# Two graph-attention layers: neighbours of 32 nodes gathered four to a tile and summed on column tiles of TensorE

## The chip, the core and the metric

The kernel runs on one core of a Trainium2 chip. The core has five engines that run side by side and wait for one another through semaphores: TensorE (PE, with its weight loads shown as PEld), VectorE (DVE), ScalarE (ACT), GpSimd (POOL) and SyncE (SP, which here only issues transfers). Sixteen DMA engines move data between DRAM and the on-chip memory SBUF. TensorE writes to a second on-chip memory, PSUM, which DVE and ACT can read. The metric is the time of one execution in microseconds, taken as the median of several runs.

## The reference

Both layers are graph attention over the same 2708 nodes with 1024 features, in f32. About 17 entries per row of the adjacency matrix are set, and a row attends only to those.

```python
def layer0(x, adj):
    f = x @ Wf + bf
    g = x @ Wg + bg
    e = relu(f @ g.T)
    a = softmax(where(adj > 0, e, NEG), axis=1)
    return a @ (x @ W + bW)

def layer1(x, adj):
    h = x @ W1
    e = leaky_relu(h @ a1 + (h @ a2).T, 0.2)
    a = softmax(where(adj > 0, e, NEG), axis=1)
    return relu(a @ h)

x = layernorm(x + layer0(x, adj))
x = layernorm(x + layer1(x, adj))
```

## The kernel before

The kernel turns the dense adjacency matrix into lists of neighbours and computes only with these. It uses that sums and products can be exchanged: f . g = x_i (Wf Wg^T) x_j plus terms with the biases, so with M = Wf Wg^T a node needs one row F = x M + c, and a score is the product of F with the row x_j of a neighbour; likewise a @ (x W) is (a @ x) W. So each layer gathers rows of x (or of the table T1 of layer 1), and multiplies by a weight matrix once per node.

*Lists (L141 to L235).* The 2708 rows are 22 blocks of 128. For each block the adjacency rows are loaded by SP, DVE multiplies them by a falling iota (L216), finds the eight largest of each of 20 segments (L220) and draws up to 40 neighbours out of these in five rounds (L224, L226). Meanwhile PE turns Wf and Wg and forms M (L200), and POOL and ACT form the products of the weights with the bias vectors and with a1 and a2 (L174, L175).

*Ranking (L237 to L298).* Nodes are sorted by their number of neighbours, so that a block needs no more places than its first node has: DVE and ACT compare every node's key with all the others (L264, L270), and POOL scatters each list to its rank in the DRAM tensor LD (L129). SP reads the ranked lists back into SL. `PLACES` says how many neighbours each block of 128 ranked nodes may have, 396 places in all. A check whether the lists fit is made here (L298 to L311); if it fails, a general path runs, which it does not for this input.

*Layer 0 (L486 to L598).* Every place is one indirect DMA of POOL (`gather_next`, L411): 128 rows of 4 KB, row p being the neighbour of node p; entries without a neighbour are out of bounds and are skipped. The tiles lie in a ring of 20 slots. A block (or half a block where it has over 20 places) is a unit. For each unit, DVE forms the score of each place as a product of the tile with F, summed along the row (`dots`, L520), `soft` (L418) makes the weights, and `add_up` (L449) sums the weighted tiles: some places on PE, as products with a diagonal 128x128 matrix of weights that ACT writes (`share`, L441), the others on DVE, one multiply-add each. `join` adds the two parts. The numbers `np0` and `np1` choose the split. A slot's next gather is issued behind the instruction that reads it last. `prepare` (L510) makes F of the block after next, `values` (L539) multiplies the sum by W, and `close` (L545) adds the residual, normalizes (`norm`, L347), forms the two products with u1 = W1 a1 and u2 = W1 a2 and scatters the row into T1.

*Layer 1 (L601 to L668).* The same with T1's rows, a ring of 28 slots, and scores that need only column D of the gathered row (`scores`, L610).

The order of the instructions on every engine in both layers is that of the code: each call is wrapped by `InOrder` (L42), so every engine works through its queue as written, and a waiting instruction holds up all that stand behind it on its engine. Since the wrapper makes these calls, the profile puts them all on L52; they are told apart by the tiles that they write and read.

## Time and profile before

| | before |
|---|---|
| median of three runs | 2166.41 us (2160.6 to 2173.15) |
| profiled execution | 2171.14 us |
| its span, first to last instruction | 2169.3 us |
| mean granted TensorE clock | 0.882 |
| busy PE, DVE, POOL, ACT | 1697.8, 1745.4, 1086.1, 461.2 us |
| moved by DMA | 501.03 MB |
| lists / ranking / start of layer 0 | 0 to 234 / 234 to 311 / 311 to 363 us |
| sums of layer 0 | 363 to 1433 us |
| between the layers | 1433 to 1501 us |
| layer 1 up to its last gather / end | 1501 to 2085 / 2085 to 2169.3 us |

The stages were read off the timeline. A line of a group names the engine and the operation, what it writes and reads (`out<-in`), how often (`x`), its busy time and mean duration, and how long its engine idled before it and for whom. `ring` is the ring of gathered tiles, `dg` a diagonal of weights, `acc` the sum on DVE, `j` the discarded product of a dot, `pm` and `pt` are PSUM tiles, `xT` and `yT` are turned rows.

### The profile page before, as it was taken

Reading aid. Unit: us, or ns where it says so; the run is one execution under the profiler, and the core shown is the slowest. Engines: PE = TensorE matmul, PEld = TensorE weight load, DVE = VectorE, ACT = ScalarE, POOL = GpSimd, SP = SyncE. Lnnn points to the kernel's source line nnn. Section 1 sums busy time; section 2 is a strip of 40 time slices with the busy share of each in tenths; the row PEclk is TensorE's granted clock in tenths of the full one; section 3 lists DMA queues with packets and bytes.
Section 4 is the critical chain, followed back from the end, with each engine's and each line's share of the span. In section 5 each row is a group of like instructions: output and inputs, shape, how many; then the busy total and the mean of one; then the engine's idle time right before and its main releaser. Section 6 shows DMA issues by size and latency. Waiting matters only on the chain.

```text
span 2169.3 us, 16547 instructions
## 1 busy us (share of the span) xinstructions
PE 1697.8 (78%) x4200; PEld 756.1 (35%) x4200; DVE 1745.4 (80%) x3089; ACT 461.2 (21%) x859; POOL 1086.1 (50%) x991
## 2 busy tenths in 40 slices
PE   2787217797788799999999999962385968886896
PEld 2343103343333334444444444320132433342442
DVE  8999836678778878989999989963677778886993
ACT  3223601111122012222222222210002212231331
POOL 4237244453453445554554454307676767775740
PEclk6799558898988899999999999975697979998998
DMA  6554027264654556765676566417898989998940
GB/s 250 202 199 162 4 89 290 82 245 164 228 205 163 199 205 250 273 249 210 235 269 259 203 233 241 149 60 276 273 362 328 350 314 378 379 371 309 378 167 34
DMA packets 143618, 501.03 MB, mean 231 GB/s; under 512 B 26040, under 2 KB 26376, under 8 KB 140806
## 3 DMA queue, kind: packets, MB, share of 16 engines
q0 software_dynamic: 125312, 424.80, 53.3%
q1 hardware_dynamic: 12088, 52.01, 6.4%
q10 hardware_dynamic: 6114, 23.07, 2.9%
q8 instruction: 36, 0.59, 0.1%
q14 instruction: 68, 0.56, 0.1%
HBM read 494.23 MB, written 33.80 MB: 243 GB/s over the span
## 4 chain that ended last, share of the span: by engine, by line
PE 42%; issue 9%; DVE 5%; another core or an unknown queue 3%; ACT 3%; DMA 3%; POOL 2%; POOLq 1%; DVEq 0%; ACTq 0%
PE pm L52 41%; DVE acc L52 2%; POOL ring L52 2%; DMA ring<-T,SL 1%; DVE j L52 1%; PE pt L52 1%; DMA more<-T,SL 1%; POOL more L52 1%; ACT F L52 1%; ACT L52 1%; POOLq L52 1%; DVE z L52 1%; DVE bst L52 0%; ACT z L52 0%
## 5 line engine op out<-in xcount | busy, mean ns | idle before, releaser
L52 POOL DMA_INDIRECT ring<-in_x_dram,SL x396 | 434.3, 1097 | 518.3 <-DVE acc L52 376.3
L52 PE MATMUL pm<-ring,dg 128*128 128x512 f32 x932 | 438.0, 626 | 157.1 <-ACT dg L52 79.1
L52 DVE SCALAR_TENSOR_TENSOR acc<-ring,sc,acc 128x1024 f32<-128x1024 f32 (+1 forms) x408 | 524.2, 1285 | 14.6
L52 DVE SCALAR_TENSOR_TENSOR j<-ring,F 128x1024 bf16<-128x1024 f32 (+1 forms) x396 | 483.7, 1222 | 22.6 <-PE pt L52 11.2
L52 PE MATMUL pm<-M,yT 128*128 128x512 f32 (+1 forms) x704 | 325.6, 622 | 73.8 <-ACT yT L52 57.1
L52 POOL DMA_INDIRECT ring<-T,SL x284 | 297.0, 1046 | 122.4 <-issue 77.5
L52 PE MATMUL pm<-Wt,xT 128*128 128x512 f32 (+1 forms) x704 | 329.5, 623 | 14.9 <-ACT xT L52 14.7
L52 PEld LDWEIGHTS pm<-ring,dg 128*128 128x128 f32 x932 | 186.2, 202 | 402.4 <-issue 312.5
L52 PE MATMUL pm<-M,xT 128*128 128x512 f32 (+1 forms) x704 | 316.8, 603 | 3.5 <-issue 3.0
L52 PEld LDWEIGHTS pm<-M,yT 128*128 128x128 f32 (+1 forms) x704 | 134.9, 195 | 251.5 <-issue 189.3
L52 PEld LDWEIGHTS pm<-Wt,xT 128*128 128x128 f32 (+1 forms) x704 | 132.4, 193 | 187.4 <-issue 167.6
L52 PEld LDWEIGHTS pm<-M,xT 128*128 128x128 f32 (+1 forms) x704 | 128.2, 187 | 166.3 <-issue 164.1
L52 POOL DMA_INDIRECT more<-T,SL x112 | 119.1, 1064 | 46.6 <-issue 30.0
L174 POOL TENSOR_TENSOR vp<-rows,vec 128x1024 f32<-128x1024 f32 x32 | 89.7, 2829 | 101.7 <-DMA rows<-in_L_gnn_Wg_dram 71.1
L52 ACT COPY xT<-pt 128x512 f32<-128x512 f32 (+1 forms) x88 | 46.9, 579 | 373.5 <-PE pt L52 233.3
L200 PE MATMUL pm<-WgT,WfT 128*128 128x512 f32 x256 | 117.1, 620 | 7.3 <-ACT M L202 6.9
L52 DVE TENSOR_TENSOR acc<-pm,acc 128x1024 f32<-128x1024 f32 x48 | 58.6, 1221 | 76.7 <-issue 47.4
L52 ACT ACT_TABLE_LOAD x79 | 101.4, 1283 | 67.9 <-DVE nm L52 49.6
L52 DVE SCALAR_TENSOR_TENSOR acc<-more,sc,acc 128x1024 f32<-128x1024 f32 (+1 forms) x82 | 105.3, 1284 | 2.9
L220 DVE MAX8 cand<-adj 128x8 f32<-128x136 f32 (+2 forms) x440 | 107.5, 281 | 0.0
L52 ACT COPY yT<-pt 128x512 f32<-128x512 f32 (+1 forms) x44 | 23.6, 570 | 327.3 <-PE pt L52 193.3
L52 ACT ACTIVATE dg<-ident,sc 128x128 f32<-128x128 f32 x258 | 81.3, 389 | 28.3 <-DVE sc L52 13.4
(126 smaller groups left out, 1317.5 us busy)
## 6 DMA issues: line engine op xcount, KB each, us to landing
adj<-in_adj_dram SPq DMA_DIRECT2D x21, 1354.0 KB
X1S<-z SPq DMA_DIRECT2D x21, 512.0 KB
x<-X1S SPq DMA_DIRECT2D x21, 512.0 KB
ring<-in_x_dram,SL POOLq DMA_INDIRECT x396
ring<-T,SL POOLq DMA_INDIRECT x284
rows<-in_L_gnn_Wf_dram ACTq DMA_DIRECT2D x8, 512.0 KB
rows<-in_L_gnn_Wg_dram ACTq DMA_DIRECT2D x8, 512.0 KB
rows<-in_L_gnn_W_dram ACTq DMA_DIRECT2D x8, 512.0 KB
```

The source lines that it names most:

```text
L52: return self.tc.keep_in_program_order(op(*args, **kwargs))
L174: nc.gpsimd.tensor_tensor(t, rows, vec, op=ALU.mult)
L200: nc.tensor.matmul(pm[:, 0, :], WfT[:, i, k * P:(k + 1) * P], WgT[:, i, :], start=(i == 0), stop=(i == KC - 1))
L220: nc.vector.max(cand[:n, s, :], k[:n, s * SEG:min((s + 1) * SEG, N)])
```

## The change

The nodes stay sorted by their number of neighbours, but the unit of the lists is now a group of 32 nodes (85 groups, 405 tiles in `TILES`), and a gathered tile holds four neighbours of each of them: row 32 q + i is a neighbour of node i. `sums` forms a group's weighted sum on PE alone: the stationary operand is a 128x32 matrix `st` (each row holds its weight in the column of its node), and the result goes to the 32 PSUM partitions that belong to the group, so the four groups of a block write to four different column tiles. Units of over 20 tiles (27 in layer 1) are cut into two units of two groups. DVE keeps the dots and writes `st`; it no longer sums. For the dots, F of a group's 32 nodes is written four times by ACT (`replicate`).

The ranks no longer come from comparing all keys: nodes fall into 11 classes by their number of tiles, counted by products with triangular and one-hot matrices, and the node of each rank is found by one-hot products (44 small ones). The lists go to DRAM unranked, block by block, and are gathered by group when they are needed (`load_lists`, 85 indirect DMAs).

Also changed: in the lists, ACT and POOL form the masked iota; the bias and a1/a2 products are formed on PE with broadcast columns, for which W1 is turned as well; weights are loaded by SP; the normalization takes its inverse root by three Newton steps on DVE and not by ACT's square root; z is one buffer; closing a block is spread over the next one by hooks in `sums`; PSUM holds two product tiles and one for the sums; layer 1's ring has 27 slots; the check of the lists comes at the end of layer 1.

```diff
-PLACES = [40, 26, 23, 22, 21, 20, 19, 19, 18, 18, 17, 17, 16, 16, 16, 15, 14, 14, 13, 12, 11, 9]
+
+TILES = [10] + [7] * 4 + [6] * 13 + [5] * 30 + [4] * 28 + [3] * 9
...
+    LD = dram.tile([N * Q, QT], I32, name="LD")
...
+    stack = const.tile([P, 32], F32, name="stack")
+    rep = const.tile([P, Q, 32], F32, name="rep")
...
+            def turned(w, k, dst):
+                t = stage.tile([P, D], F32, name="rows")
+                sp.dma_start(t, w[k * P:(k + 1) * P, :])
+                for k0 in range(0, KC, 4):
+                    pt = ps_t.tile([P, 4, P], F32, name="pt")
+                    for i in range(4):
+                        nc.tensor.transpose(pt[:, i, :], t[:, (k0 + i) * P:(k0 + i + 1) * P], ident)
+                    nc.scalar.copy(dst[:, k0:k0 + 4, :], pt)
...
+                    pm = ps_m.tile([P, H, 512], F32, name="pm")
+                    for i in range(KC):
+                        nc.tensor.matmul(pm[0:64, 0, :], bfc[:, i:i + 1].to_broadcast([P, 64]), WgT[:, i, :],
+                                         start=(i == 0), stop=(i == KC - 1))
+                        nc.tensor.matmul(pm[64:128, 0, :], bgc[:, i:i + 1].to_broadcast([P, 64]),
+                                         WfT[:, i, half], start=(i == 0), stop=(i == KC - 1))
...
+                sp.dma_start(t[:n], adj[b * P:b * P + n, :])
                 k = t.bitcast(F32)
-                nc.vector.scalar_tensor_tensor(k[:n], t[:n], 0.0, iota[:n], op0=ALU.is_gt, op1=ALU.mult,
-                                               accum_out=tot[:n, b:b + 1])
+                nc.scalar.activation(k[:n], t[:n], AF.Relu, accum_out=tot[:n, b:b + 1])
+                nc.gpsimd.tensor_tensor(k[:n], k[:n], iota[:n], op=ALU.mult)
...
-                nc.vector.tensor_scalar(PL[:n, b, 0:CAP], L[:n, b, :], -1.0, float(NONE),
-                                        op0=ALU.mult, op1=ALU.add)
+                nc.scalar.activation(PL[:n, b], L[:n, b].rearrange("p (t q) -> p q t", q=Q), AF.Relu,
+                                     scale=-1.0, bias=none[:n])
+                nc.scalar.dma_start(LD.rearrange("(n q) t -> n (q t)", q=Q)[b * P:b * P + n, :],
+                                    PL[:n, b].rearrange("p q t -> p (q t)"))
...
-                    nc.scalar.activation(j[:n], KB[:n], AF.Sign, bias=nkey[:n, b:b + 1],
-                                         accum_out=rank[:n, b:b + 1])
...
-                scatter(LD[:, :], ranki[:n, b:b + 1], PL[:, b, :], n)
-            nc.sync.dma_start(SL[:, :NB - 1, :], LD[:(NB - 1) * P, :].rearrange("(b p) c -> p b c", p=P))
...
+        pt = ps_t.tile([P, 4, P], F32, name="pt")
+        nc.tensor.matmul(pt[:, 0, :NCL], lower, sumb[:, 0, :], start=True, stop=False)
+        nc.tensor.matmul(pt[:, 0, :NCL], onesb, sumb[:, 1, :], start=False, stop=True)
...
+        for b in range(NB):
+            n = nsize[b]
+            for j in range(2):
+                nc.tensor.matmul(pt[:32, 0, :Q * NB], low4[:n, j, b, :], hot[:n, b, :],
+                                 start=(b == 0 and j == 0), stop=(b == NB - 1 and j == 1))
...
+        nc.tensor.matmul(pt[:, 0, :Q * NB], rep[:32], at32, start=True, stop=True)
+        nc.vector.tensor_scalar(idq, pt[:, 0, :Q * NB], qcol, None, op0=ALU.add)
+        for q in range(Q):
+            rows = slice(32 * q, 32 * q + 32)
+            nc.vector.tensor_scalar(ids[rows], pt[rows, 0, :Q * NB].rearrange("p (b g) -> p g b", g=Q)[:, q, :],
+                                    0.25, None, op0=ALU.mult)
...
-        act.activation(sd[:n], mv[:n, 1:2], AF.Sqrt, bias=eps[:n])
...
+        for _ in range(3):
+            dve.tensor_scalar(t[:n], var[:n], r[:n], r[:n], op0=ALU.mult, op1=ALU.mult)
+            dve.tensor_scalar(t[:n], t[:n], -0.5, 1.5, op0=ALU.mult, op1=ALU.add)
+            dve.tensor_scalar(r[:n], r[:n], t[:n], None, op0=ALU.mult)
...
+            whole = sum(TILES[g] for g in gs) <= most
+            parts = [gs] if whole else [gs[:2], gs[2:]]
...
+        def gathers(self):
+            while self.next < len(self.order) and (self.next < self.count or self.next - self.count in self.free):
+                u, g, t = self.order[self.next]
+                idx = SL[:, g, t:t + 1] if self.next >= self.count else SL0[:, g, t:t + 1]
+                gather(pool, self.rows(self.next), self.table, idx)
...
+        def soft(self, u):
+
+            sc, shape = u.sc, [P, u.G, u.T]
+            mq = small.tile([P, Q], F32, name="mq")
+            dve.tensor_reduce(mq[:, :u.G], sc, AX.X, ALU.max)
+
+            m4 = small.tile([32, Q, Q], F32, name="m4")
+            for q in range(Q):
+                dve.tensor_copy(m4[:, :u.G, q], mq[32 * q:32 * q + 32, :u.G])
+            m1 = small.tile([32, Q], F32, name="m1")
+            dve.tensor_reduce(m1[:, :u.G], m4[:, :u.G, :], AX.X, ALU.max)
+            for q in range(Q):
+                dve.tensor_copy(mq[32 * q:32 * q + 32, :u.G], m1[:, :u.G])
+            dve.tensor_tensor(sc, sc, mq[:, :u.G].unsqueeze(2).to_broadcast(shape), op=ALU.subtract)
+            act.activation(sc, sc, AF.Exp)
+            u.st = self.stp.tile([P, self.most, 32], F32, name="st")
+            dve.tensor_tensor(u.st[:, :u.G * u.T, :].rearrange("p (g t) i -> p g t i", g=u.G),
+                              sc.unsqueeze(3).to_broadcast(shape + [32]),
+                              stack.unsqueeze(1).unsqueeze(1).to_broadcast(shape + [32]), op=ALU.mult)
+            u.rs = small.tile([P, Q], F32, name="rs")
+            dve.tensor_reduce(u.rs[:, :u.G], sc, AX.X, ALU.add)
...
+        def sums(self, u, po, hooks):
+
+
+            pt = ps_t.tile([P, 4, P], F32, name="pt")
+            for k in range(u.G):
+                j = u.lo + 32 * k
+                pe.matmul(pt[j:j + 32, 0, 0:1], stack, u.rs[:, k:k + 1], start=True, stop=True)
+            u.ri = small.tile([P, 1], F32, name="ri")
+            dve.reciprocal(u.ri[u.lo:u.hi], pt[u.lo:u.hi, 0, 0:1])
+            done = 0
+            for t in range(u.T):
+                now = [(k, g, u.at + m) for m, (k, g, tt) in enumerate(u.tiles) if tt == t]
+                for h in range(H):
+                    for k, g, m in now:
+                        j = u.lo + 32 * k
+                        pe.matmul(po[j:j + 32, h, :], u.st[:, k * u.T + t, :],
+                                  self.rows(m)[:, h * 512:(h + 1) * 512],
+                                  start=(t == 0), stop=(t == TILES[g] - 1))
+                for k, g, m in now:
+                    self.free.add(m)
+                    self.gathers()
+                    for f in hooks.get(done, []):
+                        f()
+                    done += 1
...
+    def load_lists(b):
+        for g in range(Q * b, min(Q * b + Q, NG)):
+            gather(pool, SL[:, g, :], LD[:, :], idq[:, g:g + 1], N * Q)
...
+        def replicate(b, k):
+
+            Fr[b, k] = frp.tile([P, D], F32, name="Fr")
+            for p in range(Q):
+                act.copy(Fr[b, k][32 * p:32 * p + 32, :], flat(F[b])[32 * k:32 * k + 32, :])
+
+        def dots(u, lo, hi):
+            for m in range(lo, hi):
+                k, g, t = u.tiles[m]
+                dot(lay.rows(u.at + m), Fr[u.b, g - Q * u.b], P, u.sc[:, k, t:t + 1])
...
+            b = u.b
+            back = b - 1 if u.first and b > 0 else None
+            ahead = b + 2 if b + 2 < NB else None
+            hooks = {}
+            if back is not None:
+                hooks[10] = [lambda back=back: gather(pool, z[:nrows[back], :D], x, ids[:nrows[back], back:back + 1])]
+            hooks.setdefault(4, []).append(lambda s=closing: [None for _ in s])
...
+            reps = [g - Q * b for g in u.gs if g + Q < NG] if b + 1 < NB else []
+            if reps:
+                replicate(b + 1, reps[0])
+            if back is not None:
+                for _ in yTs[back][1]:
+                    pass
+            lay.sums(u, po, hooks)
+            closing = iter(())
+            for r in reps[1:3]:
+                replicate(b + 1, r)
+            act.activation(y[b][u.lo:u.hi], flat(po)[u.lo:u.hi], AF.Copy, scale=u.ri[u.lo:u.hi])
+            for r in reps[3:]:
+                replicate(b + 1, r)
+            if u.first:
+                if ahead is not None:
+                    for _ in x_turn(ahead):
+                        pass
+                if back is not None:
+                    Wp[back] = product(nrows[back], yTs.pop(back)[0], Wt, 32)
             if u.last:
-                values(u)
-                done = u.b
+                if ahead is not None:
+                    f_product(ahead)
+                if ahead is not None and ahead == NB - 1:
+                    sp.dma_start(M, W1.rearrange("(k p) d -> p k d", p=P))
+                yT = tp.tile([P, KC, P], F32, name="xT")
+                steps = turn(y[b], nrows[b], yT)
+                next(steps)
+                yTs[b] = yT, steps
+            if u.first and b + 3 < NB:
+                load_x(b + 3)
+            if u.first and b + 4 < NB:
+                load_lists(b + 4)
...
+            count = len(nxt.tiles) if nxt is not None else 0
+            part = count * 3 // 4 if u.only else count
+            half = part // 2
             if nxt is not None:
-                dots(nxt, CAP)
-                lay.soft(nxt, u)
-                lay.share(nxt, np0(nxt))
-        xr[done] = load_rows(done)
-        for _ in close(done):
+                dots(nxt, 0, half)
+            if u.first and ahead is not None:
+                q_copy(ahead)
+            if nxt is not None:
+                dots(nxt, half, part)
+            if nxt is not None and not u.only:
+                soft(nxt)
+            if back is not None:
+                closing = close(back)
+                next(closing)
...
+            if nxt is not None and u.only:
+                dots(nxt, part, count)
+                soft(nxt)
...
+        R1 = 27
...
+        over = ovp.tile([P, NG, QT], F32, name="over")
+        pool.memset(over, 0.0)
+        for g in range(NG - 1):
+            if TILES[g] < QT:
+                pool.memset(over[:, g, TILES[g]:], 1.0)
```

## The prediction

> **What bounds the kernel now.** I read the page's first part first: which engine is busy, as an average over the whole execution.
>
> ```profile
> span 2169.3 us, 16547 instructions
> PE 1697.8 (78%) x4200; PEld 756.1 (35%) x4200; DVE 1745.4 (80%) x3089; ACT 461.2 (21%) x859; POOL 1086.1 (50%) x991
> ```
>
> TensorE (PE) and VectorE (DVE) are level, so neither average says which one binds where. The busy times by stage do. I cut the span at 234 us (lists done), 311 (ranked lists read back), 363 (first weighted sum), 1433 (last sum of layer 0), 1501 (first sum of layer 1) and 2085 (last gather). Columns: stretch and its length, then busy us of PE, weight loads, DVE, ACT and POOL with counts, granted clock, DMA share, GB/s.
>
> ```profile
> 0.00:234.00 234.00, 145.66 (x384) 73.94 (x384) 224.08 (x885) 63.92 (x115) 99.17 (x45) 0.80 0.51 189
> 234.00:311.00 77.00, 12.91 (x54) 9.22 (x54) 44.16 (x71) 35.17 (x36) 24.43 (x44) 0.52 0.06 13
> 311.00:363.00 52.00, 33.90 (x86) 15.32 (x86) 30.72 (x53) 5.12 (x12) 25.37 (x24) 0.83 0.82 323
> 363.00:1433.00 1070.00, 977.48 (x2418) 428.86 (x2418) 927.74 (x1408) 212.31 (x434) 495.84 (x457) 0.95 0.58 210
> 1433.00:1501.00 68.00, 18.37 (x43) 4.14 (x42) 12.72 (x27) 5.22 (x10) 27.87 (x30) 0.63 0.57 215
> 1501.00:2085.00 584.00, 444.49 (x1049) 198.72 (x1050) 461.17 (x578) 120.91 (x226) 406.14 (x385) 0.87 0.90 336
> 2085.00:2169.30 84.30, 64.94 (x168) 25.94 (x166) 44.78 (x71) 18.59 (x28) 7.33 (x8) 0.89 0.14 48
> ```
>
> The lists are DVE's (224 of 234 us), ranking is a chain of small waits (nothing busy), layer 0 is PE's first and DVE's close behind (977 and 928 of 1070), layer 1 is the DMA's (share 0.90). What each kind of work costs is in the costliest groups (first figure busy us, then mean ns) and in the timeline of one block (start, us):
>
> ```profile
> L52 PE MATMUL pm<-ring,dg 128*128 128x512 f32 x932 | 438.0, 626 | 157.1 <-ACT dg L52 79.1
> L52 DVE SCALAR_TENSOR_TENSOR j<-ring,F 128x1024 bf16<-128x1024 f32 (+1 forms) x396 | 483.7, 1222 | 22.6 <-PE pt L52 11.2
> L174 POOL TENSOR_TENSOR vp<-rows,vec 128x1024 f32<-128x1024 f32 x32 | 89.7, 2829 | 101.7 <-DMA rows<-in_L_gnn_Wg_dram 71.1
> ```
> ```profile
> 1009.68 1.00 POOL L52 DMA_INDIRECT ring<-in_x_dram,SL  x1 [0.30 <-issue]
> 1010.99 0.99 POOL L52 DMA_INDIRECT ring<-in_x_dram,SL  x1 [0.30 <-issue]
> 1011.03 7.13 PE L52 MATMUL pm<-M,xT 128*128 128x512 f32 x16
> 1032.72 1.91 POOL L52 DMA_INDIRECT ring<-in_x_dram,SL  x1 [15.87 <-DVE acc L52]
> ```
>
> Eight f32 products appear as 16 matmul records, 0.43 us apart (7.13 us in all, each recorded 0.62 long): an f32 product of 128x512 is two passes, 0.86 us. A gather costs POOL 1.3 us (1.0 and 0.3 of issue), and waits where DVE has not yet freed a slot.
>
> **The change, part by part.**
>
> Lists. DVE has 224/22 = 10.2 us per block of 128 nodes. The masked iota product (3.40, x21) goes, with the list's cast (0.34) and one reduction (0.25); one reduction comes: 6.5 us, 143 in all. In their place ACT runs a 2708-wide pass per block (the Sign pass of that width takes 2.57) and a short one, 22 x 3.1 = 68 us beside its copies, and POOL a 2708-wide product: 2.64 x 2.83 = 7.5 us, 22 x 7.5 = 164 (136 at the 2.34 of an undisturbed pair). POOL loses the 32 vector products (89.7), so this fits. SP's queue now carries the weights too, 42 MB with the adjacency; at the 250 GB/s of the first slice 168 us, beside the rest. The lists go to DRAM by plain transfers of ACT's queue, block by block, where POOL scattered them after the ranking. PE gains most: 24 transposed weight blocks at 1.94 (47 us), the 256 passes that it has (117), and 128 new passes for the bias rows and W1's two vectors (0.46 each, 59): 223 us, from 14 us on. The ranking's first product stands behind them: about 230 us, bounded by 180 (POOL) and 245.
>
> Ranking. The 77 us stage (22 wide comparisons, 22 scatters 2.7 us apart, a read back) becomes some 20 DVE operations over about 7,000 elements in all, at the 1.2 ns per element of the 880-wide row, and 47 small products with four handovers: 15 us. Then four list gathers (5.2, plus about 3 to land) stand ahead of the rows on POOL, and ACT's first spread of F (four copies of 32x1024, at the 1.06 of a 128x1024 pass) ahead of the first dot: 60 where 52 were. First sums: 230 + 15 + 60 = **305** where 363 were; 270 to 330.
>
> Layer 0. 405 tiles take the place of 396 places. Per block (18.4 tiles): DVE loses its share of sums (10 to 11 of 18 at 1.29) and the joins (1.22), keeps 18.4 dots at 1.27 (23.3), two products with u1 and u2 and one with rb (3.8), residual add and statistics (2.7), and gains the Newton steps (about 14 at 0.15, 2.0) and a soft of some 16 small operations with one 640-wide product (3.5): 35 us. ACT: 16 copies of F at 1.06 (17), five of 0.6, two wide ones: 24; the 79 table loads (101 us) mostly go, all off the path. POOL: 18.4 gathers, four of lists, two of rows, one scatter, 25.7 x 1.3 = 33 us. The lists' gathers come last in a block's queue and the tiles' ahead of them; z is one buffer now, so its refill waits for its scatter, with tile gathers queued behind, up to the 2.5 us by which a scatter lands after its issue. Slots now come free when PE has summed them, not DVE, and in order: the next block's gathers, and behind them its dots, begin as the sums end.
>
> PE: two products by M and Wt (14.7 each), 16 transposes (2.1), small products and handovers (2): 33.5, and the sums, S. Alone, they are 405 x 2 halves x 2 passes x 0.43 = 697 us per layer, 31.7 per block. No row shows two matmuls at once, so S is bounded by this from above and by a quarter from below, four products in turn writing four different groups of 32 outputs. In the five widest blocks (126 tiles, two units each) only two column groups are in use: 126 x 0.86 + 279 x 0.43 = 228 us, S = 10.4. I take this end: weights, rows and outputs of neighbours in PE's order are all different, so nothing of the data makes one wait for the next, and the weight loads (0.19) already hide under the passes. With 1.5 us of coupling, layer 0 is 22 x (33.5 + 10.4 + 1.5) = **999** where 1070 were. PE, DVE and POOL stand within ten us: freeing DVE buys little.
>
> [...]
>
> Layer 1. Gathers are what it waits for already: 215 GB/s x 68 us and 336 GB/s x 584 us are 211 MB, and the same rows are fetched (places that hold no neighbour are skipped before and after). At the 364 GB/s of its best stretch (1800 to 2000) that is 580 us, at 336 it is 628; POOL's 427 issues at 1.31 are 559. DVE, nearly free now, buys nothing. From the first gather, 30 us after the last sum, I take 600. PE (14.0 + 2 + S = 8.7, only block 0 being in two units) stays below. The end: three blocks drained in 84 us; one does now, 45 (sums, transposes, 14.0 product, norm 6, scatter), and the check of the lists is moved behind the last scatter: 83 memsets at 0.056, two 850-wide DVE passes, a product, a copy, about 8. Layer 1: 30 + 600 + 53 = **683** where 736 were.
>
> Sum: 305 + 999 + 683 = 1987. The profiled execution took 2171.1 us for a span of 2169.3 and stands 4.7 above the median of 2166.4: 1987 + 1.8 - 4.7, about **1985**.
>
> **The rivals.** *Pairs only (slower).* The two passes of a product use the same column group, so if PE starts matmuls in order, pass two of one product overlaps only pass one of the next: 0.86 us a tile, S = 15.8 in both layers. For it: every pass in the trace starts 0.43 after the one before. Against: no row has column groups. Layer 0 is 22 x 50.8 = 1118, layer 1 PE's, 68 + 22 x 33 + 53 = 847 (14.0 + 2 + 15.8 + 1.2 a block): 305 + 1118 + 847 = 2270; without any coupling 2210. I put it at 2240. The sign turns at 305 + 22 x (35 + S) + 121 + 22 x (17 + S) = 2169, S = 13.6, an overlap of 2.3.
>
> *No overlap, the change not doing what it says.* S = 31.7: 305 + 22 x 66.7 + 121 + 22 x 48.7 = 2965. For it: all that the trace shows of PE is one pass after another. Against: a product with 32 columns leaves three quarters of the array unused.
>
> *Better than the sum.* PE and POOL without coupling (966), the lists ending with POOL's products (180, so first sums at 255), gathers at 364 GB/s (30 + 580 + 53): 1884. Against: engines within ten us of each other rarely run without waits.
>
> **How the numbers follow.** Fourfold overlap, 0.58, with its own range 1900 to 2090 (first sums at 270 to 330, coupling 0 to 4 us a block, the DMA rate); better 0.05; pairs 0.27; none 0.10. 1850 to 2260 leaves out none (0.10), the upper part of pairs (0.06) and what lies under 1850 (0.03). About 0.5% is what a measurement here tells from no change. Faster: 0.57 + 0.05 + a fifth of pairs 0.05 = 0.67; within 0.5%: 0.03; slower: 0.30.
>
> **What would show it.** Matmuls of 128*32 in four groups: start to start of four neighbours near zero and a round of four tiles in about 1.8 us, not 3.4 or 6.9. PE's busy time between first and last sum of layer 0 near 960 of 1000. First sum at 305; no table loads; POOL gathers waiting for PE, not DVE; layer 1 at a DMA share of 0.9 with DVE mostly idle. Wrong would make it: pairs; POOL's 33 us becoming the bound because list gathers or the z refill hold up tiles; the ranking not waiting for PE.

## The result

The changed kernel takes 2437.28 us (median of four, 2419.97 to 2447.02) where the kernel before, beside it, takes 2163.6 (median of four): a ratio of 1.125, with an interval of 1.117 to 1.132. It is slower by an eighth; the forecast was 1985 us. The profiled execution took 2447.02 us. Some executions of a kernel take over 1.5% longer than its fastest, and the ratios in this document leave those out.

The first part of its page, busy time of each engine, against the same lines of before:

```profile
span 2445.3 us, 22226 instructions
PE 1807.8 (74%) x6982; PEld 718.1 (29%) x6982; DVE 1180.3 (48%) x3547; ACT 638.2 (26%) x769; POOL 1191.0 (49%) x1147
```

DVE lost 565 us of work and PE gained 110, and both have a lower share than before: no engine is busy for more than 74% of the span, so the time went into waiting. The busy times by stage say where (stretch and length, busy us of PE, weight loads, DVE, ACT and POOL with counts, granted clock, DMA share, GB/s). The first three rows hold the lists and the ranking, which end at 284 and 306 us; 412.5 is the first sum, 1640 lies 25 us behind the last sum of layer 0, 1722 where layer 1 is under way, 2347 at the last gather.

```profile
0.00:255.00 255.00, 179.63 (x578) 88.94 (x578) 125.85 (x660) 105.37 (x144) 125.42 (x63) 0.87 0.45 166
255.00:300.00 45.00, 0.36 (x2) 0.13 (x2) 44.48 (x183) 5.98 (x9) 28.11 (x13) 0.50 0.06 13
300.00:355.00 55.00, 23.99 (x96) 13.38 (x97) 5.50 (x15) 17.21 (x19) 37.77 (x39) 0.69 0.78 284
355.00:412.50 57.50, 19.36 (x44) 8.31 (x43) 25.90 (x54) 1.39 (x3) 44.40 (x44) 0.62 0.13 22
412.50:1640.00 1227.50, 994.18 (x3560) 381.93 (x3561) 749.50 (x1738) 429.18 (x482) 523.58 (x473) 0.88 0.53 185
...
1722.00:2347.00 625.00, 480.40 (x2347) 188.13 (x2344) 177.83 (x707) 63.91 (x93) 380.34 (x383) 0.87 0.87 305
2347.00:2445.30 98.30, 74.38 (x252) 28.30 (x247) 34.97 (x129) 12.48 (x17) 10.58 (x95) 0.91 0.15 55
```

In layer 0 the shares of PE (from 91% to 81%), DVE (87% to 61%) and POOL (46% to 43%) have fallen, and the granted clock from 0.95 to 0.88; only ACT has more to do, 35% for 20%. No stage reached its forecast:

| stage | before | forecast | after | missed by |
|---|---|---|---|---|
| up to the first sum | 363 | 305 | 412.5 | 107 |
| layer 0, first to last sum | 1070 | 999 | 1203.0 | 204 |
| last sum of layer 0 to the end | 736 | 683 | 829.8 | 147 |

**The sums themselves do what the forecast took.** The timeline of PE through one full block of layer 0 (start, us, and in brackets the idle time before and who ended it), and that of ACT:

```profile
1002.71 0.59 PE L53 MATMUL pt<-qd,rep 128*128 128x4 f32 x2 [5.04 <-ACT xT L53]
...
1003.76 9.05 PE L53 MATMUL pm<-Wt,xT 128*128 128x512 f32 x16
...
1013.05 7.13 PE L53 MATMUL pm<-Wt,xT 128*128 128x512 f32 x16
...
1040.91 0.29 PE L53 MATMUL pt<-rs,stack 128*32 128x1 f32 x8 [5.09 <-ACT xT L53]
1041.04 10.81 PE L53 MATMUL po<-ring,st 128*32 128x512 f32 x80
1051.79 1.09 PE L53 MATMUL pt<-ident,xb 128*128 128x128 f32 x8
1057.92 0.59 PE L53 MATMUL pt<-qd,rep 128*128 128x4 f32 x2 [5.04 <-ACT xT L53]
```
```profile
1036.11 0.22 ACT L53 ACTIVATE scores<-scores 128x20 f32<-128x20 f32 x1 [7.53 <-DVE scores L53]
1036.23 4.02 ACT L53 COPY Fr<-pm 32x1024 f32<-32x1024 f32 x4
1040.28 1.07 ACT L53 COPY xT<-pt 128x512 f32<-128x512 f32 x2
```

The 80 passes of a block of 20 tiles take 10.81 us. One after another at 0.43 they would take 34.4, in pairs 17.2, four at once 8.6. Inside the row four passes start 3 to 7 ns apart and the next four 0.43 us later; only the first five rounds are about 0.85 apart. So in this row column tiles overlap four deep, both passes of an f32 product included.

**What is lost is around them.** The block takes 55.2 us (1002.7 to 1057.9): products 31.6, transposes and small ones 2.9, sums 10.8, and two waits of 5.0 and 5.1 us for a copy of ACT. PSUM has two buffers for `pt`; the transposes take both, and the product with `qd` or `rs` behind them needs a third, so it waits until ACT has copied a turned tile out. ACT is busy only a third of this stage (429 of 1227 us), but that copy stands in its queue behind four copies `Fr<-pm` (4.02 us here), and these behind an exponential that waited for DVE's scores until 1036.11. After each wait PE runs some 4 us at half speed, with a granted clock of 0.51 from 1003.7 to 1007.7 and from 1041.0 to 1045.3 us and of 1.00 behind either stretch: the first sixteen passes (eight products) take 9.05 us, the next sixteen 7.13, and five rounds of the sums about 0.85 us each. The waits of PE in layer 0 and of POOL in layer 1 (us in total, times, longest), first PE's:

```profile
PE pt L53 <- ACT xT L53: 176.5, 36, 18.6
PE pt L53 <- DVE j L53: 53.8, 5, 38.1
```
```profile
POOL ring L53 <- PE po L53: 96.3, 43, 11.1
POOL more L53 <- PE po L53: 19.8, 11, 7.0
```

A wait need not be of 5 us for slow passes to follow it. In e16 (below) PE waited 1.36 us, with short transposes ahead of it and small products behind it, and the next sixteen passes took 8.83 us for 7.13 all the same:

```profile
844.89 1.09 PE L53 MATMUL pt<-ident,xb 128*128 128x128 f32 x8
847.34 0.39 PE L53 MATMUL pt<-qd,rep 128*128 128x4 f32 x2 [1.36 <-ACT xT L53]
847.66 0.38 PE L53 MATMUL pm<-rows,ones 3*128 3x512 bf16 x1
847.97 8.83 PE L53 MATMUL pm<-Wt,xT 128*128 128x512 f32 x16
```

What makes the passes slow after so short a wait is not shown here. The forecast counted no slow passes: it had 1.5 us a block for all coupling.

In layer 1 POOL stands 116 us for slots that PE has not freed. In the kernel before, POOL's waits for slots in that stage were 20.5 us for PE and 16.5 for DVE.

### The profile page after: what moved, and what is told of

Read it like the earlier page. It is cut to its first block, busy times and chain, and to the rows that moved or that the text cites. A ratio compares the mean times of both kernels' runs of the same rounds, so it can differ in the third digit from the quotient of the medians.

```text
span 2445.3 us, 22226 instructions
## 1 busy us (share of the span) xinstructions
PE 1807.8 (74%) x6982; PEld 718.1 (29%) x6982; DVE 1180.3 (48%) x3547; ACT 638.2 (26%) x769; POOL 1191.0 (49%) x1147
## 5 line engine op out<-in xcount | busy, mean ns | idle before, releaser
L53 DVE SCALAR_TENSOR_TENSOR j<-ring,Fr 128x1024 bf16<-128x1024 f32 x405 | 496.5, 1226 | 164.9 <-DMA ring<-in_x_dram,SL 146.6
L53 PE MATMUL po<-ring,st 128*32 128x512 f32 x2820 | 536.5, 707 | 14.9 <-issue 14.7
L53 ACT COPY Fr<-pm 32x1024 f32<-32x1024 f32 x340 | 341.0, 1003 | 69.2 <-PE po L53 29.1
L53 PE MATMUL pm<-Wt,xT 128*128 128x512 f32 (+1 forms) x704 | 349.7, 654 | 6.4 <-ACT xT L53 6.4
L53 PEld LDWEIGHTS po<-ring,st 128*32 128x32 f32 x2820 | 136.1, 129 | 338.2 <-issue 335.8
L53 POOL DMA_INDIRECT T<-z,ids x22 | 27.1, 1231 | 397.2 <-issue 283.6
L284 POOL TENSOR_TENSOR adj<-adj,iota 128x2708 f32<-128x2708 f32 (+1 forms) x22 | 129.8, 5927 | 129.6 <-ACT adj L283 128.6
L53 PE MATMUL po<-more,st 128*32 128x512 f32 x420 | 182.0, 704 | 1.4 <-issue 1.3
L53 ACT ACTIVATE z<-z,sh,rstd 128x1024 f32<-128x1024 f32 (+2 forms) x44 | 54.3, 1235 | 474.0 <-DVE sh L53 474.0
L53 ACT ACTIVATE y<-po,ri 128x1024 f32<-128x1024 f32 (+2 forms) x50 | 55.6, 1112 | 363.9 <-PE po L53 260.2
```

The costliest lines, as they stand in the source:

```text
L53: return self.tc.keep_in_program_order(op(*args, **kwargs))
L284: nc.gpsimd.tensor_tensor(k[:n], k[:n], iota[:n], op=ALU.mult)
```

## The experiments

The runs were made in five groups, each with runs of the kernel before on the same chip, on which it took 2193, 2177, 2087, 2088 and 2087 us (e1 to e4, e5 to e8, e9 to e12, e13 to e16, e17 and e18). So ratios are compared across groups, and times inside one. Stage times are from each run's profile; that of layer 0 holds across groups (1198 to 1214 us in the seven runs that leave it as in the changed kernel). The rest does not: the changed kernel itself had its first sum at 412.5 us in its first run and at 382.0 in e13 below, and from first to last sum of layer 1 it took 695.3 and 638.4. The edits are shown shortened: lines are joined, and guards and some arguments are left out.

**Is the overlap real, and are the sums on the path?** e2 sums group by group, so that neighbours in PE's order use the same column tile; e3 makes every pass twice.

```diff
e2  -for t in range(u.T):            # round by round over the groups
    +for own in range(u.G):          # all tiles of one group, then the next
e3  -for h in range(H):
    +for h, e in [(h, e) for h in range(H) for e in range(2)]:
```

> The same products, but a unit's sums go group by group, so that neighbours in TensorE's order write the same 32 output columns. Theory A (four neighbours of different column groups really run at once; in the trace their records start 3 to 7 ns apart, a round of four every 0.43 us): without it a product of 512 columns takes its two passes of 0.43 us alone, a unit of 20 tiles 34 us in place of 11, the sums of a layer 697 us in place of 309 and 251; the whole rises by 22 x 18 to 22 x 24 us in layer 0 and 22 x 10 to 22 x 20 in layer 1, to 3050 to 3350 us. Rival B (the records are only listed side by side and the array works on one after the other): nothing changes, 2437.

> Every product of the sums is done twice, and the sums of the weights too, so that the quotient is what it was. Theory A (TensorE's work sets the block in layer 0; in layer 1 the loop of gathers does, of which only the first round of the sums is a part): layer 0 rises by what the sums take, some 230 to 300 us, layer 1 by some 60 to 120 (a first slot comes free 1 to 2 us later, and the sums begin to outrun what they hide behind), the whole 2437 to 2730 to 2860. Rival B (loops through ScalarE, VectorE and the gathers set both layers, TensorE has slack): under 100 us in all. Rival C (sums decide in both layers alike): 560 us, the whole about 3000.

e2 took 3016.35 us, ratio 1.375 [1.362, 1.387]. The timeline of PE in e2, a block of the same size:

```profile
1065.64 32.05 PE L53 MATMUL po<-ring,st 128*32 128x512 f32 x80
```

32.05 us where the same 80 passes took 10.81: the first six start about 0.85 us apart, most others 0.43. Layer 0 took 1550 us for 1203. That settles the rival of pairs: alternating the column groups is worth a factor of three here. (Against the 8.77 us of e9 below it is 3.65, but that row has no slow passes at its start.) The condition of that rival, PE starting matmuls in order so that pass two of a product overlaps only pass one of the next, was a supposition of the author's, and no run shows it hold f32 products to pairs: in the changed kernel four passes start 3 to 7 ns apart and the next four 0.43 us later.

e3 took 2769.91, ratio 1.263 [1.251, 1.274]. All spans of sums together grew by 252 us in layer 0 (309 to 561) and by 189 in layer 1 (251 to 440); layer 0 grew by 244 and the stretch from first to last sum of layer 1 by 91. In layer 0 a microsecond more of sums is nearly a microsecond more of the stage; in layer 1 it is half of one.

**Is it ScalarE's order in layer 0?** e1 moves the copies that PE waits for ahead of `Fr<-pm`; e5 also closes a block behind the next block's softmax and holds T's scatter and the refill of z back; e9 is e5 with the copies of the turned y ahead of the z activation; e14 is e9 with only 8 of the 16 copies of Fr (in place of 12) ahead of y and of the copies of the turned x.

```diff
e1  -if reps: replicate(b + 1, reps[0])
     for _ in yTs[back][1]: pass                 # copies of the turned y
    +if reps: replicate(b + 1, reps[0])
     lay.sums(u, po, hooks)
     ...
     act.activation(y[b][u.lo:u.hi], flat(po)[u.lo:u.hi], AF.Copy, ...)
    -for r in reps[3:]: replicate(b + 1, r)
     for _ in x_turn(ahead): pass                # copies of the turned x
    +for r in reps[3:]: replicate(b + 1, r)
e5  -hooks.setdefault(4, []).append(lambda s=closing: [None for _ in s])
     dots(nxt, 0, 3)
    +for _ in shut: pass                         # shut = the closing of the block before
    -part = count * 3 // 4 if u.only else count  # dots ahead of close(back)
    +part = count
e9   soft(nxt)
    +if u.last:
    +    for _ in yTs[b][1]: pass
     closing = close(back)
e14 -for r in reps[1:3]: replicate(b + 1, r)
    +for r in reps[1:2]: replicate(b + 1, r)
    -for r in reps[3:]: replicate(b + 1, r)
    +for r in reps[2:]: replicate(b + 1, r)
```

> Layer 0 only: ScalarE copies the two transposes of a block out of PSUM ahead of the spreading copies of F, where they stood behind four of these. In the changed kernel TensorE waits 5.1 us twice in a block of 20 tiles for exactly these copies, and after each wait its passes start 0.85 us apart for some 4 us. Theory A (this in-order wait is what a block of layer 0 costs over the forecast): 10.1 us of waiting and about 3.8 us of slow passes go from each of 17 full blocks, some half of that from the five wide ones; layer 0 1203 to about 1000, the whole 2437 to about 2230. Rival B (the loop of gathers: last sums, gathers, last dots, softmax, next sums, takes 52 of the block's 55 us, so that TensorE's waits are only slack of that loop): 3 us a block, the whole about 2370.

> Layer 0 only. The order of ScalarE's copies as in the run before it, and also: VectorE does the next block's last five dots, its softmax and the dot with r ahead of the closing of the block before, and GpSimd's scatter to T and refill of z are held back behind the tile gathers by small VectorE copies of their index. Theory A (after ScalarE's order the loop sums, gathers, dots, closing, softmax, sums is what sets 52 us a block: 5 us from the sums to the first steady gather, 32 of gathers, 2.5 to land, 6 of closing and 6.5 of dots behind the last of them, 3.8 of softmax): 6 us of closing and some 4 of the scatter and refill leave that loop, TensorE's own 44 to 47 us set the block; layer 0 goes from 1106 to 980 to 1030 us, the span 2338 to 2210 to 2260. Rival B (TensorE's products and transposes already set the 52, with the slow passes after each wait): layer 0 within 20 us of 1106.

> As the run that put VectorE's last dots and softmax ahead of the closing (layer 0 1128 us, no better than ScalarE's order alone with 1106), and in ScalarE's order the copies of y's transposes also stand ahead of the closing's normalisation. In that run they stood behind it: TensorE, done with its products at 1008.3 us, waited 4.1 us for them, ScalarE waiting for VectorE's closing, and then ran slow passes for 4 us. Theory A (every engine's order must let TensorE go on; with this one TensorE sets the block): TensorE's waits fall from 8 to under 3 us a block, a full block from 52 to 45 to 48 us, layer 0 to 1000 to 1060 us, the span to 2250 to 2300. Rival B (the loop of gathers at 1.4 us a tile sets 50 to 52 us whatever TensorE does): layer 0 within 25 us of 1106.

> The order of e9_layer0, with eight of the sixteen copies of Fr per block moved behind the copies that TensorE's third pt waits for. Theory A (ScalarE's order is all that is left of the loss in layer 0): the wait of 5.4 us a block goes, a full block takes 43 to 45 us for 49, layer 0 about 1010 us for 1112, and the time falls by 90 to 110 us against e9_layer0, to a ratio of 1.03 to 1.05 to before. Rival B (the loop of gathers and dots, sums to freed slots to 20 gathers to dots to softmax, is already the next bound at 47 to 48 us): layer 0 falls by 20 to 40 us only, ratio 1.065 to 1.08.

e1: 2339.42, ratio 1.065 [1.059, 1.072]; layer 0 1105.6 for 1203, and the two waits 2.6 and 4.0 us in a block for 5.0 and 5.1. One reordering gave back 97 us of the 204, about half of what theory A said. The second wait stays since the copies still stand behind the exponential, which waited for DVE's scores until 1050.30 while PE had been ready since 1047.6.

e5: 2339.52 us in one run and 2378.64 to 2380.02 in three, of which one is the profile, with layer 0 at 1127.8. So it has no ratio with an interval; even its fastest run is at about 1.075 of the 2177 of the kernel before: no gain over e1 can be seen, a miss. The z activation, which waits for DVE's closing, now stood ahead of the copies of the turned y, and PE's wait stayed at 4.1 us. One queue had been mended by blocking another.

e9: 2261.73, ratio 1.083 [1.081, 1.085]; layer 0 1112.5, about 49 us a full block, where 1000 to 1060 was expected: a miss, and the number that its rival gave. Timelines of PE and of ACT in e9:

```profile
1027.39 8.77 PE L53 MATMUL po<-ring,st 128*32 128x512 f32 x80
...
1042.61 0.59 PE L53 MATMUL pt<-qd,rep 128*128 128x4 f32 x2 [5.43 <-ACT xT L53]
```
```profile
1028.77 12.17 ACT L53 COPY Fr<-pm 32x1024 f32<-32x1024 f32 x12
```

The wait ahead of the sums is gone, and with it their slow rounds: 8.77 us is twenty rounds of 0.43. The other wait remains, since twelve copies of Fr (12.17 us) now outlast the sums. So the rival's reason, a loop of gathers, is not needed for its number.

e14: 2214.14, ratio 1.062 [1.059, 1.064]; layer 0 1058.2, 54 us less than e9 by moving copies alone. To compare with it in the same group, the changed kernel itself was run again:

> The changed kernel itself once more, beside the next three, because the kernel before took 2087 to 2201 us from chip to chip and so each comparison needs its own. If what costs the change its time is the order of its instructions alone, its ratio to before stays near 1.125 (1.10 to 1.15). If it is something of the chip (the stretches in which TensorE issues one instruction per 0.70 us), the ratio moves by more than that with the chip.

e13: 2369.78, ratio 1.136 [1.134, 1.138], layer 0 1210.7. So the loss is nearly the same where the kernel before is 76 us faster. From e13 to e14 layer 0 falls by 152 us and the time by 156. In the two, PE's waits for ACT in layer 0 are 166.3 and 74.9 us. Full blocks now take 44.0 us and 48 to 50 in turn: neither theory is quite right, since the wait goes in every second block only.

**What holds every second block?** In e16 (below), which has e14's layer 0, the refill of z landed 4.1 us after DVE wanted it in the long blocks, and DVE's closing, the z activation and the copies of Fr were late in turn. e17 puts T's scatter, the rows of a later block and the refill of z ahead of that block's four list gathers.

```diff
e17 -if u.first and b + 3 < NB: load_x(b + 3)
    -if u.first and b + 4 < NB: load_lists(b + 4)
     dots(nxt, 0, 3)
     for _ in shut: pass                         # scatter of T
    +if u.first and b + 3 < NB: load_x(b + 3)
     dots(nxt, 3, half)
     gather(pool, z[...], x, iz[...])            # refill of z
    +if u.first and b + 4 < NB: load_lists(b + 4)
```

> e16_joined_rounds with GpSimd's order in layer 0 changed: the scatter of T, the rows of a later block, the refill of z and only then that block's lists, behind the 20 gathers of the ring. In e16 full blocks took 44.0 and 51.7 us in turn; in the long ones the refill of z landed 4.1 us after VectorE wanted it, the z activation stood 7.9 us later than in the short ones, the Fr copies behind it, and TensorE waited 1.7 and 6.3 us for the copies behind those. Theory A (that refill is the cause of the long blocks): all full blocks take 44 to 45 us, layer 0 falls from 1049 to 990 to 1010 us, ratio 0.965 to 0.975. Rival B (the loop of gathers, dots and softmax, 20 gathers of 1.3 us, 20 dots of 1.27 us and the closing, needs 47 to 48 us of VectorE a block): layer 0 1030 or more, ratio 0.985 or more.

e17: 2043.89 us beside 2087.38, ratio 0.980 [0.978, 0.982]: layer 0 1018.1 for e16's 1048.6, long blocks 47 to 49 us for 48 to 54. That lies between the two theories: part of each long block's wait (4.3 us for `xT`, 57.2 in all of layer 0) is still there.

**Layer 1: the ring's order, its slots, or the bytes?** Tiles are gathered group by group, but freed round by round, so a gather waits for a slot that comes free late. e6 gathers in the order of the rounds, e7 has 30 slots besides; e11 fetches only half of each row (2 KB for 4, so layer 1 computes with other numbers) and e12 does that in e7's order.

```diff
e6  +u.tiles.sort(key=lambda x: (x[2], x[0]))    # layer 1: by round, then group
e7  -R1 = 27
    +R1 = 30
e11 -gather(pool, self.rows(self.next), self.table, idx)
    +gather(pool, self.rows(self.next)[:, :514], T1[:, :].rearrange("n (h c) -> (n h) c", h=2), idx)
```

> Layer 1 only: the tiles of a unit lie in the ring round by round (first neighbours of all four groups, then second ones) as the sums use them, where they lay group by group. Theory A (gathers go in ring order, sums free slots in round order, so the next unit's first gathers wait for one slot a round; GpSimd stands some 7 us a block for sums in the changed kernel): GpSimd's waits for sums in layer 1 fall from 116 us to about 70 (the first round stays, 3.4 us at the slow passes), layer 1 from its first gather to its last, 680 us, to 610 to 640, the span 2445 to about 2390. Rival B (transfers at 305 GB/s or the softmax between gathers and sums set it): within 15 us of 2445.

> As the run before it, with 30 slots in layer 1 in place of 27 (one buffer each for the rows of x1, for y and for its transpose). Theory A (the ring is short: a unit of 20 tiles leaves 7 slots for gathers ahead, and the loop first sums, the 13 other gathers, landing, softmax, sums takes 31 to 33 us where GpSimd's 21 transfers take 27): 10 slots ahead take 3 x 1.3 us out of that loop, so another 2 to 4 us a block, the span some 2320 to 2360; the DMA share of layer 1 goes from 0.87 towards 0.95. Rival B (something else sets the 33 us): no more than 15 us under the run before it.

> Layer 1 of the changed kernel with half the bytes: each gather fetches 514 of 1028 numbers a row, from another row, and the score is one of these, so sums and scores of layer 1 are of other numbers; instructions, slots and the neighbours skipped are the same. Theory A (the loop GpSimd's 1.3 us a transfer, the wait for the first freed slot and the softmax sets layer 1): 680 us from first gather to last stay within 30. Rival B (transfers set it: DMA share 0.87): it falls by 80 us or more, to what GpSimd issues, 427 x 1.3 = 555, plus at most some waits.

> The same halving with the ring in round order and 30 slots. With whole rows that kernel took as long in layer 1 as the changed one, though GpSimd's waits for sums fell: instead TensorE issued one instruction in 0.70 us, waiting for nothing that the profile shows, in 161 us of stretches behind some ten back to back gathers, and what waits for its last sums waited with it. Theory A (those stretches come with the load of the transfers, and take back what the slots gave): with half the bytes they are gone and layer 1 falls to GpSimd's 27 to 29 us a block, 600 to 630 us from first gather to last. Rival B (they come with the number of gathers issued back to back, not with bytes): they stay, and layer 1 stays above 650.

e6 took 2450.13, ratio 1.128 [1.116, 1.139], e7 2453.08, 1.129 [1.118, 1.140]: no gain, but not for the reason that the rival gave. In both, PE went through stretches in which the products and weight loads on record started 0.70 us or a multiple of it apart and waited for nothing that the profile shows: some 90 to 115 us in e6, by how such a stretch is counted, and about 160 in e7, mostly in layer 1, against 25 to 29 us in the changed kernel, most of it in the first unit of layer 0, and 20 in the one before. They can hide what the order gives. In the last three groups none was seen, so the question was put again there.

e11 took 2325.26, ratio 1.114 [1.112, 1.116], and e12 2307.97, 1.106 [1.104, 1.108]. From first to last sum of layer 1: 639 in e9 (same group, whole rows), 588 in e11, 567 in e12. Half the bytes are worth 51 us in the old order, which lies between e11's two theories, and with half the bytes the new order is still worth 21 us. No such stretch was seen in this group with whole rows either (e9), so e12 does not show that bytes were behind them.

e16 is e7's order without halved rows, on top of e15 (below):

> e15_joined_split, and layer 1's ring in the order of the rounds with 30 slots. Theory A (in layer 1 GpSimd waits for freed slots, since tiles are gathered by group and freed by round; e6_rounds and e7_rounds_more gained nothing because stretches of slow issue took the gain): where those stretches are absent, first to last sum of layer 1 falls from 638 to about 600 us, ratio 0.02 lower than e15_joined_split. Rival B (GpSimd's 1.3 us a gather is the bound in either order): within 0.005 of e15_joined_split.

e16: 2074.58, ratio 0.993 [0.991, 0.995], 57 us less than e15; first to last sum of layer 1 583.4 for 636.9. Waits of POOL in layer 1, of e13:

```profile
POOL ring L53 <- PE po L53: 64.2, 46, 10.4
POOL more L53 <- PE po L53: 9.5, 8, 4.4
```

and of e16:

```profile
POOL ring L53 <- PE po L53: 15.2, 22, 6.3
POOL more L53 <- PE po L53: 13.7, 13, 5.2
```

So the new order with three more slots takes 54 us off layer 1, and fewer bytes take about as much off the old order (51). The two do not add: in the new order whole rows take 583 us and half rows 567. With order and slots as in e16 little is left for the bytes to give; as the change had them, bytes counted too. No run without such stretches separates the order from the slots.

**The first sum.** Three things were late here. The lists ended at 284 us, with PE's weights done at 217: SP sends adjacency blocks and W1's rows in one queue, and a row waits for a staging buffer that PE has to empty. Queue of SP in the changed kernel (`rows<-in_L_gnn_W_dram` are W1's rows), and what others waited for up to the first sum:

```profile
48.37 0.88 SPq L53 DMA_DIRECT2D adj<-in_adj_dram  x1
111.37 0.33 SPq L53 DMA_DIRECT2D rows<-in_L_gnn_W_dram  x1
...
118.81 0.47 SPq L53 DMA_DIRECT2D adj<-in_adj_dram  x1
181.56 0.33 SPq L53 DMA_DIRECT2D rows<-in_L_gnn_W_dram  x1
```
```profile
POOL adj L284 <- ACT adj L283: 128.6, 10, 47.5
ACT PL L294 <- DVE L L291: 75.5, 19, 6.4
ACT M L240 <- PE pm L238: 41.5, 10, 6.3
DVE j L53 <- DMA xb<-in_x_dram,ids: 38.0, 2, 35.2
```

For 63 us no adjacency block went out, and from 119 to 182 us again none. Later the rows of block 1 were asked for at 349 us, behind the 20 gathers of the ring and the lists of blocks not yet needed, and DVE stood 35.2 us for them with its own dots behind. e4 holds each block's lists back by a copy of their index on DVE and asks for block 1's dot only after half of block 0's; e8 moves W1's rows behind block 13, and the list's last step from ACT to DVE and SP; e10 is e9 with both; e15 is e14 with both, W1's rows behind all blocks, and the residual rows of the last blocks and the check of the lists earlier.

```diff
e4  +dve.tensor_copy(iq[:, :c], idq[:, Q * b:Q * b + c])
     for k in range(c):
    -    gather(pool, SL[:, g, :], LD[:, :], idq[:, g:g + 1], N * Q)
    +    gather(pool, SL[:, Q * b + k, :], LD[:, :], iq[:, k:k + 1], N * Q)
e8  -nc.scalar.activation(PL[:n, b], L[:n, b]..., AF.Relu, scale=-1.0, bias=none[:n])
    +nc.vector.tensor_scalar(PL[:n, b], L[:n, b]..., -1.0, float(NONE), op0=ALU.mult, op1=ALU.add)
    -for _ in range({0: 0, 1: 8, 2: 4, 3: 4}.get(b, 1)): next(steps, None)
    +for _ in range({1: 8, 2: 4, 3: 4}.get(b, 1 if b > 12 else 0)): next(steps, None)
e15 -for _ in range({1: 8, 2: 4, 3: 4}.get(b, 1 if b > 12 else 0)): next(steps, None)
    +for _ in range({1: 8, 2: 4, 3: 4}.get(b, 0)): next(steps, None)
    +load_x(0)
     load_lists(0)
    -load_x(0)
    +residual(b, frp, "Fr")                      # last blocks: rows of x not through z
```

> The gathers of the lists are held to one block's at a time by a small VectorE copy of their index, and the rows of block 1 and its dot with r come after half of block 0's dots; in the changed kernel about 60 list gathers (78 us of GpSimd) stand in one piece between 340 and 430 us, ahead of the tiles of the second unit, and VectorE's dots stand from 318 to 354 us behind the rows of block 1. Theory A (these two are most of the 106 us from the ranked lists to the first sums, where 60 were forecast, and of the first unit's 39 us): first sums at 365 to 380 in place of 412, the first unit 15 to 20 us in place of 39, the whole 2437 to 2360 to 2385. Rival B (the list gathers fill time in which GpSimd has nothing else, and the start waits for something else): the whole within 15 us of 2437.

> List stage only: the negated list of a block is made by VectorE, as in the kernel before, and stored by SyncE four blocks later, where ScalarE did both in order between its Relu passes and the copies of the weights; and W1's rows enter SyncE's queue from block 13 on, where they entered from block 4 on and held up the adjacency from 48 to 111 us and again to 181. Theory A (the in-order queues of SyncE and ScalarE, not the work, put the end of the lists at 282 us: GpSimd is busy 125 of 255 us and VectorE 126): lists at 6.6 us a block end at 170 to 200, TensorE's 217 us then bound the ranking, first sums at 330 to 350 in place of 412, the whole 60 to 80 us less. Rival B (the lists must share GpSimd, VectorE and the DMA with the weights anyway): less than 20 us.

> The layer 0 of the run before this one, the list stage with the negated lists on VectorE and their stores on SyncE, and the list gathers held to one block's at a time. Theory A (the three are independent): first sums 357 (list stage) less 45 (start) = 312 us, layer 0 as in the run before this one, the rest 830: 2140 to 2200 us in all, about level with the kernel before. Rival B (the list stage then ends with TensorE's weights at 217 us and the ranking behind them, so the two gains overlap): first sums at 330 to 345, 2170 to 2240.

> e14_layer0_split, the lists held at their place (as e4_lists_late), the rows of block 0 fetched ahead of the first lists, the start of the lists without W1's rows in between (W1 after all blocks of adj), the residual rows of the last three blocks fetched ahead, and the check of the lists done during layer 1. Theory A (the three losses that the traces show, before the first sum, in layer 0 and at the seams, are separate and add): first sum about 300 us (323 in e10_joined), layer 0 about 1000, the seam between the layers 45 us for 52, the end 8 us shorter: 60 to 90 us faster than before on this chip's kernel would need all of it; ratio 0.97 to 1.00. Rival B (they are not separate, the loop of gathers takes what ScalarE gives): ratio 1.03 to 1.045.

e4: 2413.09, ratio 1.100 [1.091, 1.108]; first sum 367.7, and the first unit's sums 17.3 us, for 412.5 and 39.2 in the changed kernel (382.0 and 20.1 in e13); layer 0 then took 1222.0, and the time missed the 2360 to 2385 that was expected. e8: 2386.62, ratio 1.097 [1.089, 1.105]; first sum 357.1; what W1's place and the list's last step each gave was not separated. e10: 2182.84, ratio 1.046 [1.044, 1.048]; first sum 323.3 for 381.7 in e9, 58 us, less than e4's 45 and e8's 55 together. e15: 2131.62, ratio 1.020 [1.017, 1.023]: first sum 321.0 for e14's 383.3, and 9 us less after layer 0. The gain here is that of e10 again; the later W1 bought nothing, because of what e16's timeline of DVE shows:

```profile
252.29 0.41 DVE L340 TENSOR_TENSOR eq<-eq,pt 128x242 f32<-128x242 f32 x1 [31.95 <-PE pt L334]
```

The lists were done at 212 us, and then the ranking stood 32 us for its first product, which PE had queued behind W1. e18 puts the ranking first and fetches five of W1's rows ahead of the last adjacency blocks:

```diff
e18 -for _ in steps: pass                        # all of W1, then the ranking
    +next(steps)
    +ranking()
    +for _ in steps: pass
```

> e17_refill_early with the ranking ahead of W1's two products, and five of W1's rows fetched before the last blocks of adj. In e16 the lists were done at 212 us, but the ranking's first product stood on TensorE behind W1 until 252 (VectorE waited 32.0 us for it). Theory A (the ranking waits for TensorE's queue, as a rival of the prediction had it): first sum falls from 322 to about 295 to 300 us, the time by 20 to 25 us against e17_refill_early. Rival B (W1's second half and the memory that it holds push the first gathers instead): first sum 310 or later, under 12 us gained.

e18: 2040.04, ratio 0.979 [0.975, 0.982], no gain over e17 that the intervals tell, first sum 323.2 for 321.7. The ranking ended 30 us earlier, at 233 (e16: 263), but the first rows of x were asked for only at 254, since POOL waited 14.7 us for PE to turn W1's last rows, and the ring's at 262 behind them. The rival was right: W1 is in the way in either place.

**A version that beats both.** e17 and e18 are level: the change, with its instructions in another order, a few steps on another engine and three more slots in layer 1, takes 2.0% less than the kernel before (1.8% to 2.2%). The kernel before was not put in a better order itself; what that would give it is not shown. e17's busy times by stage, cut at the first sum, the last sum of layer 0, and the first and last sum of layer 1:

```profile
0.00:321.70 321.70, 226.80 (x718) 111.15 (x720) 229.19 (x937) 122.72 (x151) 189.28 (x108) 0.86 0.51 183
321.70:1339.80 1018.10, 917.96 (x3519) 365.82 (x3519) 749.48 (x1771) 421.66 (x478) 556.80 (x522) 0.94 0.64 223
1339.80:1415.10 75.30, 30.86 (x85) 10.82 (x86) 23.70 (x78) 4.93 (x7) 27.13 (x28) 0.73 0.50 185
1415.10:1997.50 582.40, 518.35 (x2599) 205.42 (x2597) 200.48 (x832) 72.28 (x105) 404.64 (x488) 0.94 0.92 348
1997.50:2042.20 44.70, 28.65 (x74) 10.04 (x74) 11.17 (x39) 5.21 (x7) 2.85 (x3) 0.86 0.09 30
```

DVE and ACT do in layer 0 what they did in the changed kernel (749 and 422 us, for 750 and 429), PE's busy time is smaller at the higher clock (918 for 994), and the clock is at 0.94 for 0.88. It is the waits that went.

## Why the prediction was wrong

*Fourfold overlap: right.* S was put at 228 us in layer 0 (10.4 a block) and at 8.7 a block in layer 1 (its own terms give 8.5, 187 us), from the lower bound. The units' spans sum to 309 and 251 in the changed kernel, where the first rounds are at half speed and the first unit alone takes 39.2, and to 252.6 and 226.9 in e9. A round of four tiles takes 4 x 0.43 = 1.7 us, as the sign said. The rival of pairs, at 2240, lay nearer to the measured time, but for a cause that is not there; the rival of no overlap is what e2 builds, and it took 3016. That 2965 was said is close by luck: e2's first sum came 104 us later than in that sum, its layer 0 took 83 more, and the rest 141 less.

*Layer 0, "with 1.5 us of coupling": the step that failed most.* In a full block the other terms hold: 31.6 + 2.9 for 33.5, 10.8 for 10.4. Coupling is 10.1 us of waits; with the 2 us by which each slows what follows, which stand inside the other terms, a full block takes 55.2 us for the 45.4 that were summed. The forecast had counted ACT's work (24 us a block) and called it "all off the path". Its amount is; its order is not. PE waits for one particular copy in the middle of ACT's queue, because `pt` has two buffers and three users. Moving copies alone gave back 97 us of layer 0 in e1, and another 54 from e9 to e14. Of the rest, the late refill of z is 30 us (e17 against e16), and e17 still shows 1018 for 999.

*Lists: "230", measured 284.* PE was given 223 us of work from 14 us on and was done at 217, but it was not busy for all of that (180 us in the first 255): the 128 new passes ran two at a time in two column tiles, 7.09 and 8.83 us for 32 of them, and the rest was waiting. So that number is near in part by luck. The ranking did not wait for PE, which the forecast had named as a sign against it; "bounded by 180 (POOL) and 245" was a bound by amounts of work. The missing term was again a queue: W1's rows ahead of adjacency on SP, twice 63 us without a block. The forecast said that SP's queue "now carries the weights too" and gave it 168 us "beside the rest", without asking for which buffer each row waits. POOL's product took 5.9 us for the 7.5 said, so POOL was never near.

*Ranking: "15", measured 22 (284 to 306).* The estimate went by elements; in the timeline five operations of DVE took 1.0 to 2.3 us that their size does not explain (`hl`, 128x22, took 1.99 us, and the next one, alike, 0.16). POOL was at casts and sums of its own then, and `hl` ended as one of these did (295.6 us). In e16, where POOL had finished before, the same two took 0.18 and 0.17 us: the long time of `hl` is seen only beside POOL's work (2.11 us from 293.49). That this work was in the way is an estimate from these rows.

*Start: "60", measured 106.* The forecast counted four list gathers ahead of the rows and nothing between them and the first dots. But block 1's rows came behind the ring's gathers and eight more lists, its dot stood ahead of block 0's on DVE, and more than 50 list gathers of 1.3 us each then held POOL until about 430. Holding the lists back brings the first sum to 368 in e4; with the list stage changed too, it comes at 321 to 323 in e10 and e15. Some 30 us are not the kernel's order at all: the same kernel had its first sum at 382.0 in e13.

*Layer 1: "30 + 600 + 53", measured 53 + 679 + 98.* The 600 was worked out from bytes and from POOL's issues, and first to last gather in 573 us (e16) and 571 (e17) shows that it could be had. Of the 79 us over it, 51 are not the kernel's order: in e13 the same kernel took 628, and no run says why. What was left out in the other 28 is that slots come free in another order than they are filled; that order, with three more slots, is worth more than these (54 us from first to last sum, e16 against e15). The 53 for the end took one block to be drained; when the last gather is issued at 2347, PE is still in the sums of the block with 12 tiles that began at 2345, and two more follow at 2369 and 2390, since 27 slots hold two blocks of 12 tiles and the one of 3. The 53 between the layers is three closings in a row through one z buffer, each with scatter and refill (1611.6, 1640.8 and 1664.8 us); the forecast knew of this refill and charged it 2.5 us.

*The signs.* What was said would show the change right held in part: no POOL gather waits for DVE's sums, the 79 table loads of the layers are gone, the share of DMA in layer 1 is 0.87 (0.9 said), DVE is mostly idle there (178 of 625 us busy). "PE's busy time near 960 of 1000" gave 994 of 1227: the first number was near, the second not. No sign named ACT: the rival of a wait that takes the place of the removed one was not worked out for the engine with the least work.

Stage by stage the forecast was what the change could reach: 305, 999 and 683 us were said, 321.7, 1018.1 and 702.4 are reached in e17. It was a forecast of the work, not of this order of it, and the miss is one of order: the work took what was said wherever its order let it.

## What to carry to other kernels

For every engine that hands a buffer on, ask not how much work it has but what stands in its queue ahead of the one instruction that others wait for, and how many users share its buffers; in a kernel whose queues are written by hand such order, with three more slots and a few steps moved to another engine, was worth 326 us of 2370 (e13 to e17, in two groups where the kernel before agrees within 1 us). Charge a wait of TensorE with the slow passes that follow it: here one of 5.0 to 5.1 us cost another 2 (9.05 us for 7.13, 10.81 for 8.77), and one of 1.36 us cost 1.7 more in e16. Fill a ring in the order in which it is emptied.

## What was not expected of the hardware

- Four column tiles ran side by side in f32, where each product is two passes: 80 passes in 8.77 us at the higher clock (10.81 with slow rounds at the start), against 32.05 (slow passes at the start included) with neighbours in the same column tile.
- After a wait of about 5 us TensorE worked at half speed for about 4 us (0.85 us a round for 0.43, 9.05 us for 7.13, the granted clock 0.51 for 1.00). After one of 1.36 us, between short transposes and small products, it did so too (8.83 us for 7.13).
- In some runs the products and weight loads of TensorE that are on record started 0.70 us or a multiple of it apart for a while, waiting for nothing that the profile shows: in the changed kernel 1.40 us apart from 418.5 to 435.2 us, then loads at 435.95, 436.65 and 437.35; in e7 products at 2009.32, 2010.71 and 2012.13. In the stretches looked at (e6 and e7) POOL issued ten or more gathers back to back meanwhile. In all, such stretches take 25 to 29 us in the changed kernel and about 160 in e7; none was seen in the last three groups, with the same gathers (e13 is the changed kernel itself). The cause stays open.
- Two operations of DVE, alike and of 128x22, took 1.99 and 0.16 us where POOL worked beside the first, and 0.18 and 0.17 in e16, where POOL was done.
- The kernel before took 2193 us in the first group and 2087 in the last, on a chip of the same number. No run here says why; the ratio of the changed kernel moved only from 1.125 to 1.136.
